# Layernorm, attention and ternary FFN on one core: head 1's keys and queries by seven block products, the second group's values in the lead-in

## The chip, the core and the metric

The kernel runs on 1 core of a Trainium2 chip. A core has TensorE (PE; its weight loads are listed as PEld), VectorE (DVE), ScalarE (ACT), GpSimd (POOL) and SyncE (SP, which here issues DMAs), an on-chip SBUF, and PSUM, where matmuls put their results. Each engine works through its own queue in order and waits on semaphores. The metric is device microseconds of one execution; before the change the median of 3 runs was 2255.35 us (2254.96 to 2256.19).

## What is computed

All in float32, with x of 2048 rows and 256 columns, 16 heads of 128, and a hidden FFN width of 704. The input x, of one batch, is normalized once; attention and FFN both read the normalized rows, and both are added to x.

```python
xn = _layernorm(x, axis=-1)
x = x + attn(xn, Wqkv, Wout) + ffn(xn, w1, w2, w3)

# attn
qkv = jnp.einsum('bsd,ed->bse', x, Wqkv).reshape(B, S, 3 * H, D)
q, k, v = qkv[:, :, :H], qkv[:, :, H:2 * H], qkv[:, :, 2 * H:]
logits = jnp.einsum('bqhd,bkhd->bhqk', q, k) * D ** (-0.5)
w = softmax(logits)
out = jnp.einsum('bhqk,bkhd->bqhd', w, v).reshape(B, S, H * D)
return jnp.einsum('bse,de->bsd', out, Wout)

# ffn: each weight matrix rounded to -1, 0, 1 times the rows
x1, x2 = _bitlinear(x, w1), _bitlinear(x, w2)
return _bitlinear(sigmoid(x1) * x2, w3)
```

## The kernel before

**Stages.** The front loads x and the first weights, normalizes x, and turns it into `xnT`, which has 128 of the 256 columns on the partitions twice (KC = 2), and all 2048 rows along it. In its gaps PE makes values of the first group of heads and queries of head 0. A group is G = 2 heads. Then the FFN runs over four chunks of 512 rows, with keys of head 0 between its first chunks. Then comes attention.

**Attention's loop.** A block is one head and 512 queries (NB = 4 blocks a head, 64 in all); a block has TB = 4 tiles of 128 queries. One turn of the loop at L733 makes the scores of tile v = u + 6 and the weighted sums of tile u, so that scores run LEAD = 6 tiles ahead. The turns with u < 0 (v = 0 to 5) are the lead-in: they have scores and no weighted sums, and other products fill PE instead, by the table `first` (L726). This text calls the turn that makes the scores of tile v "step v".

In a step, in this order: scores of tile v in two halves of 1024 keys (L602, two products each), a maximum of each half on DVE (L607) and the negated one of both (L612); `beside`, which may put a block product on PE and its read on DVE; the exponentials of both halves on ACT (L619); pieces of keys, queries or values; the first weighted sums (L660); a second block product; DVE's transposes of tile v - 2 (L650); the second product's read; the exchange of tile v by 16 DMAs of 64 KB (L634, ten on SP's queue, six on ACT's), which the transposes two steps later wait for; the remaining weighted sums. The order is written out by hand (`tc.manual_schedule`): each engine gets its instructions in the order of the program, and a DMA also waits for the DMA eight before it.

Score tiles have three buffers of two PSUM banks (`ps_s`). The other two banks are `ps_m` and `ps_av`, one buffer each. Pieces take their bank by `bank` (L87), in the lead-in and before by turns and later always `ps_m`, while block products always take `ps_m`:

```python
pool, tag = ((ps_m, "m"), (ps_av, "av"))[len(banks) % 2] if lead_in else (ps_m, "m")
banks.append(name)
```

**Pieces.** `k_piece` (L99) and `q_piece` (L111) make 128 x 512 of keys or queries by two products of 512 columns, which ACT copies out of PSUM (L109, L120). `v_piece` (L216) makes 256 rows of values for both heads of a group by four products of 256 columns, copied by ACT (L228). A float32 product is two instructions on PE. Head 0's keys and queries, and head 1's, are made by pieces: eight pieces of 512 columns a head. Head 1's fall into steps 1 to 4, 9 and 13.

**Seven block products.** For heads 2 to 15, keys and queries of two chunks of 512 rows are four outputs, each a sum of two products, eight in all; the kernel makes them by seven, from sums of weights (`weight_sums`, L133, POOL) and sums of x (`x_sums`, L143, POOL, once). `fast_product` (L151) puts one product into `ps_m`; `fast_read` (L168) adds it on DVE to one or two outputs (L185, L188, L192) and `fast_scaled` (L207) makes a scaled copy (L211). A pair of chunks is spread over four steps: (b, i) = (0,0), (0,1), (1,0) with two products each, (1,1) with one. Here b is the block in its pair and i the first or second tile of the block. A step with two has the first beside the scores and the second after some weighted sums. Values of groups 2 to 7 are made in a similar way (`fast_v_product`, L251).

**Around it.** `load_weights` (L72) starts a DMA of a group's weights. Each kind of weight has one buffer, so that a load waits until the last product that reads the old ones is done. Group 1's value weights are loaded in step 1 by SP, in its queue between the exchange of tile 0 with the FFN's last result (`yd`, L517) and the exchange of tile 1. Group 1's `wq` and `wk` are loaded by POOL in steps 12 and 14 (L81). `x_sums` are in step 1 and lie in a pool that takes the place of the FFN's.

Of the kernel before, what the change touches and what calls it, by code (L numbers as in the profile page):

```python
# [19 lines left out]
def layernorm_attention_bitffn_kernel(  # L20
# [78 lines left out]
    def k_piece(h: int, c: int):  # L99
        if c == 0:  # L100
            kTs[h] = kvpool.tile([P, S], F32, tag="kT", name=f"kT{h}")
        w = weights[h // G, "k"]
        pm = bank([P, QB], f"pk{h}_{c}")
        for d in range(KC):
            nc.tensor.matmul(  # L105
                pm, w[:, d, bass.ts(h % G, D)], xnT_k[:, d, c],
                start=(d == 0), stop=(d == KC - 1),
            )
        nc.scalar.copy(kTs[h][:, bass.ts(c, QB)], pm)  # L109
# [410 lines left out]
    with tc.manual_schedule():  # L520
        nc.gpsimd.memset(ones, 1.0)

        idle = ps_s.tile([P, 2, QB], F32, tag="s", name="idle")
        for i in range(20):
            nc.tensor.transpose(idle[:, i % 2, :P], ident, ident)
        with tc.tile_pool(name="fraw", bufs=1) as fraw:
            raw = loads(fraw)

            normalized(fraw, 0, 0, 2)
            turned(0, 0, 2)  # L530
            normalized(fraw, 0, 2, TB)
            v_piece(0, 0)
            turned(0, 2, TB)
            normalized(fraw, 1)
            q_piece(0, 0)
            v_piece(0, 1)
            turned(1, 0, 2)
            turned(1, 2, TB)
            normalized(fraw, 2)
            magnitude(fraw, 0, raw[0])  # L540
            v_piece(0, 2)
            q_piece(0, 1)
            magnitude_of_all(0)
            v_piece(0, 3)
            turned(2, 0, 2)
            turned(2, 2, TB)
            normalized(fraw, 3)
            quantize(fraw, 0, raw[0])
            magnitude(fraw, 1, raw[1])
            v_piece(0, 4)  # L550
            q_piece(0, 2)
            magnitude_of_all(1)
            turned(3)
            quantize(fraw, 1, raw[1])
            magnitude(fraw, 2, raw[2])
            v_piece(0, 5)
            v_piece(0, 6)
            q_piece(0, 3)
            magnitude_of_all(2)
            halved_x(0)  # L560
            quantize(fraw, len(raw) - 1, raw[-1])
        for c in range(2):
            k_piece(0, c)
        fp = front.enter_context(tc.tile_pool(name="ffn", bufs=2))
        chunks = [(c, f) for c in range(NB) for f in range(FC)]
        for i, (c, f) in enumerate(chunks):
            hidden(fp, c, f)
            if f == 2 and c + 1 < NB:
                halved_x(c + 1)
            if i < 2:  # L570
                k_piece(0, i + 2)
            else:
                summed(fp, *chunks[i - 2])
            if f == 3 and c:
                added(c - 1)

        warm = small.tile([P, 1], F32, tag="warm", name="warm", bufs=1)
        nc.scalar.activation(warm, ident[:, 0:1], AF.Exp)
# [139 lines left out]
    def put_away(n: int):  # L718
# [5 lines left out]
    GB = G * NB  # L724

    first = {  # L726
        1: [("v", 0, NV - 1), ("k", 1, 0)], 2: [("k", 1, 1), ("k", 1, 2)],
        3: [("k", 1, 3), ("q", 1, 0)], 4: [("q", 1, 1), ("v", 1, 0)], 5: [("v", 1, 1), ("v", 1, 2)],
    }
    made = {p for todo in first.values() for p in todo}  # L730
    moved = None
    with tc.manual_schedule():
        for u in range(-LEAD, (NBK - 1) * TB):  # L733
            n, t = divmod(u, TB)
            v = u + LEAD
            lead_in = u < 0
            more = v < NBK * TB
            h, b = blocks[v // TB] if more else (H, 0)


            seven = 2 <= h + 1 < H and v % TB < 2
            hi = h + 1, b, v % TB
            product, read, twice = fast_product, fast_read, (b % 2, v % TB) != (1, 1)

            if t == 0 and n >= GB and n // GB + 1 < H // G:
                seven = True
                hi = n // GB + 1, n % GB
                product, read, twice = fast_v_product, fast_v_read, n % NB != NB - 1


            moving = None
            if n >= GB and n // GB + 1 < H // G and n % NB > 1:
                moving = n // GB + 1, n % GB // NB, int(n % NB == 2)
            pms = []

            def beside():
                if v == 0:

                    for c, f in chunks[-2:]:
                        summed(fp, c, f)  # L760
                if seven:
                    pms.append(product(*hi, False))
                    read(*hi, False, pms[0])

            if more:
                scores(v, amid=(lambda: added(NB - 1)) if v == 1 else None, late=beside)

            if lead_in:
                for what, hg, i in first.get(v, ()):
                    {"q": q_piece, "k": k_piece, "v": v_piece}[what](hg, i)  # L770
                if v == 1:
                    front.close()
                    apool = ctx.enter_context(tc.tile_pool(name="apool", bufs=2))
                    load_weights(1, "v")
                    for c in range(0, NB, 2):
                        x_sums(c)
            elif t == 0:
                if n < GB and ("v", 1, n) not in made:
                    v_piece(1, n)
            elif t == 1:  # L780
                if n:
                    inverses(n - 1)
                    projected(n - 1, 0)
                if n % GB == GB - 1 and n // GB + 2 < H // G:
                    load_weights(n // GB + 2, "v")
            elif t == 2:
                if n and n % GB == 0:
                    load_weights(n // GB, "o", nc.gpsimd)
                if n % GB == GB - 1 and n // GB + 2 < H // G:
                    v_sums(n // GB + 2)  # L790
            if h == 0:
                if v % TB == 0 and ("k", 1, b) not in made:
                    k_piece(1, b)
                elif v % TB == 1 and ("q", 1, b) not in made:
                    q_piece(1, b)
            if b == NB - 1 and h + 2 < H:
                if h % G == 0 and v % TB in (0, 2):
                    load_weights(h // G + 1, "qk"[v % TB // 2], nc.gpsimd)
                if v % TB == 3:
                    weight_sums(h + 2)  # L800
            first_of_pair = product is fast_product and (b % 2, v % TB) == (0, 0)
            twice = seven and twice
            ahead = KQ // 2 if first_of_pair else KQ - 1
            if u >= 0:
                for k in range(t * KQ, t * KQ + ahead):
                    weighted(n, k)
            if twice:
                pms.append(product(*hi, True))
            if u == (NBK - 1) * TB - 1:
                inverses(NBK - 2)  # L810
                inverses(NBK - 1)
            if v > 1 and v - 2 < NBK * TB:
                transposed(v - 2)
            if twice:
                read(*hi, True, pms[1])
            if seven and first_of_pair:
                fast_scaled(h + 1, b)
            if more and t != TB - 1:
                exchanged(v)
            if u >= 0:  # L820
                for k in range(t * KQ + ahead, (t + 1) * KQ):
                    weighted(n, k)
            if more and t == TB - 1:
                exchanged(v)
            if u >= 0 and t == 1 and n:
                projected(n - 1, 1)
            if moving and t == 1:
                v_exchanged(*moving)
                moved = moving
            elif moved and t == 0:  # L830
                v_transposed(*moved)
                moved = None
            if t == 2 and n >= 0:
                if n:
                    put_away(n - 1)
                fetched(n)
                if n == NBK - 2:
                    fetched(NBK - 1)

        n = NBK - 1  # L840
        for k in range(NKT):
            weighted(n, k, 0)
            if k in (KQ - 1, 3 * KQ - 1):
                projected(n - 1, k // (2 * KQ), ps_s, "s")
        for k in range(NKT):
            weighted(n, k, 1)
            if k == KQ - 1:
                projected(n, 0, ps_m, "m")
        projected(n, 1, ps_s, "s")
# [38 lines left out]
```

## Time and profile before

| what | us |
|---|---|
| median of 3 runs (lowest, highest) | 2255.35 (2254.96, 2256.19) |
| the profiled execution, whole | 2257.09 |
| its span, from the first instruction to the last | 2255.3 |
| PE busy in the span | 2244.7 |
| DVE, ACT, POOL busy | 1681.3, 692.8, 317.8 |
| front and FFN, up to the first scores | 0 to 105.3 |
| lead-in, from the first scores to the first weighted sums | 105.3 to 152.1 |

The costliest groups of instructions; each row has the line, engine, operation, output and inputs, shapes and count, then busy us in all and mean ns of one, then idle us of the engine just before them and what ended it:

```profile
L619 ACT ACTIVATE p<-s,nm 128x1024 f32<-128x1024 f32 x512 | 566.0, 1110 | 1436.8 <-DMA part<-p 986.3
L607 DVE TENSOR_REDUCE mx<-s 128x1 f32<-128x1024 f32 x512 | 626.8, 1225 | 448.8 <-PE s L602 448.6
L660 PE MATMUL av<-pT,v 128*128 128x512 f32 (+1 forms) x2080 | 940.2, 586 | 0.7 <-DVE pT L650 0.7
L602 PE MATMUL s<-kT,qT 128*128 128x512 f32 x2048 | 921.9, 592 | 1.6 <-ACT p L619 1.5
L650 DVE STREAM_TRANSPOSE pT<-part 128x1024 f32<-128x1024 f32 x512 | 604.8, 1219 | 29.4 <-DMA part<-p 27.6
```

Matmuls overlap: the mean of 592 ns counts from the start of one to its own end, and the starts of two that follow each other are closer. In a timeline, a row gives start, us, engine, line, operation and count, and in brackets the idle time before it and what ended it. In a row of windows, each engine's busy us stands with its number of instructions; the granted TensorE clock (1.00 is full), the DMA engines' busy share and GB/s end the row.

### The profile page before, as it was taken

To read this page: it belongs to the slowest core of one execution; us is meant where nothing else is said; L and a number is where in the kernel's file an instruction comes from. 1 tells how busy PE (TensorE), PEld (TensorE's weight loads), DVE (VectorE), ACT (ScalarE), POOL (GpSimd) and SP (SyncE) were. 2 spreads that over 40 slices of the span, in tenths; PEclk is the share of its full clock that TensorE was granted. 3 is DMA by queue.
4 is the path that set the end of the run, shared out by engine and by line. 5 is a ranking of instruction groups with operands and counts; after the bars stand their busy time and mean duration, and the time that the engine had idled before them with its cause. 6 is when DMAs were issued, how large, how long until landed. Compare 5 with 4: busy or idle time off the path is not lost.

```text
span 2255.3 us, 24534 instructions
## 1 busy us (share of the span) xinstructions
PE 2244.7 (100%) x5754; PEld 1086.1 (48%) x5754; DVE 1681.3 (75%) x2205; ACT 692.8 (31%) x1203; POOL 317.8 (14%) x625
## 2 busy tenths in 40 slices
PE   9999999999999999999999999999999999999999
PEld 6744444444444444444444444444444444444445
DVE  6566777777777777777777777777777777777775
ACT  5533323223223223323323322322322322232331
POOL 0010000021030211203022120222103021120000
PEclk9999999999999999999999999999999999999999
DMA  2066665665665665666666665666666666666665
GB/s 95 28 164 160 171 162 147 175 176 151 166 182 152 180 174 149 177 173 167 160 175 157 176 181 147 166 179 173 168 159 174 166 174 164 157 176 173 168 170 155
DMA packets 237793, 364.73 MB, mean 162 GB/s; under 512 B 74576, under 2 KB 82192, under 8 KB 237648
## 3 DMA queue, kind: packets, MB, share of 16 engines
q1 hardware_dynamic: 131120, 178.36, 31.9%
q10 hardware_dynamic: 74704, 101.68, 17.8%
q0 software_dynamic: 31824, 83.13, 12.0%
q8 instruction: 45, 0.74, 0.1%
q14 instruction: 100, 0.82, 0.1%
HBM read 46.20 MB, written 35.65 MB: 36 GB/s over the span
## 4 chain that ended last, share of the span: by engine, by line
PE 94%; DMA 2%; SPq 1%; DVE 1%; ACT 1%; issue 0%; ACTq 0%; DVEq 0%
PE s L602 37%; PE av L660 37%; PE pw L165 7%; PE po L686 5%; PE pvw L263 3%; DMA part<-p 2%; PE ph L467 2%; PE pv L222 1%; PE pf L490 1%; SPq L634 1%; ACT p L619 0%; PE pq L115 0%; DVE pT L650 0%; PE pk L105 0%; ACTq L634 0%
## 5 line engine op out<-in xcount | busy, mean ns | idle before, releaser
L619 ACT ACTIVATE p<-s,nm 128x1024 f32<-128x1024 f32 x512 | 566.0, 1110 | 1436.8 <-DMA part<-p 986.3
L607 DVE TENSOR_REDUCE mx<-s 128x1 f32<-128x1024 f32 x512 | 626.8, 1225 | 448.8 <-PE s L602 448.6
L660 PE MATMUL av<-pT,v 128*128 128x512 f32 (+1 forms) x2080 | 940.2, 586 | 0.7 <-DVE pT L650 0.7
L602 PE MATMUL s<-kT,qT 128*128 128x512 f32 x2048 | 921.9, 592 | 1.6 <-ACT p L619 1.5
L650 DVE STREAM_TRANSPOSE pT<-part 128x1024 f32<-128x1024 f32 x512 | 604.8, 1219 | 29.4 <-DMA part<-p 27.6
L660 PEld LDWEIGHTS av<-pT,v 128*128 128x128 f32 x2080 | 395.1, 190 | 456.3 <-issue 449.9
L602 PEld LDWEIGHTS s<-kT,qT 128*128 128x128 f32 x2048 | 388.6, 190 | 464.8 <-issue 452.5
L287 POOL DMA_DIRECT2D xnT<-v x384 | 189.2, 501 | 346.5 <-DVE v L295 236.4
L721 POOL DMA_DIRECT2D yd<-ya x60 | 33.6, 560 | 735.3 <-DVE ya L693 734.0
L686 PE MATMUL po<-wo,oT 128*128 128x256 f32 x512 | 131.7, 380 | 0.6 <-DVE oT L669 0.5
L686 PEld LDWEIGHTS po<-wo,oT 128*128 128x128 f32 x512 | 97.0, 190 | 67.8 <-issue 58.4
L693 DVE SCALAR_TENSOR_TENSOR ya<-po,ri,ya 128x256 f32<-128x256 f32 x256 | 111.9, 479 | 18.0 <-issue 2.5
L619 ACT ACTIVATION_READ_ACCUMULATOR p<-s,nm 128x1 f32 x512 | 100.2, 196 | 0.0
L165 PE MATMUL pw<-t,ws 128*128 128x512 f32 x168 | 85.9, 593 | 0.0
L715 POOL DMA_DIRECT2D ya<-yd x64 | 34.3, 536 | 306.4 <-DMA yd<-ya 238.5
L188 DVE TENSOR_TENSOR kT<-pw,kT 128x512 f32<-128x512 f32 x112 | 74.7, 667 | 0.2 <-issue 0.2
L612 DVE TENSOR_REDUCE nm<-mx 128x1 f32<-128x2 f32 x256 | 39.7, 155 | 28.2 <-DVE mx L607 1.4
L185 DVE SCALAR_TENSOR_TENSOR qT<-pw,qT 128x512 f32<-128x512 f32 x84 | 57.4, 684 | 0.0
L165 PE MATMUL pw<-xnT,wk 128*128 128x512 f32 x112 | 57.2, 592 | 0.0
L280 DVE TENSOR_TENSOR v<-pvw,v 128x512 f32<-128x512 f32 x84 | 56.1, 680 | 0.0
L672 ACT COPY oT<-av 128x512 f32<-128x512 f32 x64 | 37.3, 583 | 59.2 <-PE av L660 53.6
L165 PEld LDWEIGHTS pw<-t,ws 128*128 128x128 f32 x168 | 31.6, 189 | 40.7 <-issue 33.7
(113 smaller groups left out, 784.8 us busy)
## 6 DMA issues: line engine op xcount, KB each, us to landing
part<-p SPq DMA_DIRECT2D x2560, 64.0 KB, 2.1
part<-p ACTq DMA_DIRECT2D x1536, 64.0 KB, 2.2
ya<-yd POOLq DMA_DIRECT2D x64, 512.0 KB, 4.2
yd<-ya POOLq DMA_DIRECT2D x60, 512.0 KB, 4.1
xnT<-v POOLq DMA_DIRECT2D x384, 32.0 KB, 2.6
wv<-in_wqkvT_dram SPq DMA_DIRECT2D x8, 256.0 KB, 3.6
yd<-y SPq DMA_DIRECT2D x4, 512.0 KB, 2.6
wq<-in_wqkvT_dram POOLq DMA_DIRECT2D x7, 256.0 KB, 3.7
```

The lines of the kernel that those rows point to most:

```text
L165: nc.tensor.matmul(pm, lhs, rhs, start=True, stop=True)
L185: nc.vector.scalar_tensor_tensor(q, pm, SCALE, base, ALU.mult, ALU.add)
L188: nc.vector.tensor_tensor(k, pk, base, ALU.add)
L263: nc.tensor.matmul(pm, lhs, rhs, start=True, stop=True)
L287: nc.gpsimd.dma_start(v_part[q // 2][bass.ts(j, 32), bass.ts(q % 2, S // 8)], v[bass.ts(q, 32), bass.ts(j, S // 8)],)
L602: nc.tensor.matmul(s[:, bass.ts(j, QB)], qTs[h, b][:, bass.ts(t, P)], kTs[h][:, i * HALF + j * QB : i * HALF + (j + 1) * QB], start=True, ...
L607: nc.vector.tensor_reduce(mx[:, i : i + 1], s, AX.X, ALU.max)
L619: nc.scalar.activation(p, s, AF.Exp, bias=nm, accum_out=sums[n][:, t, i : i + 1],)
L650: nc.vector.transpose(pTs[n][:, t, 2 * i : 2 * i + 2], part)
L660: nc.tensor.matmul(av, vs[h // G, k // (NKT // 2)][:, h % G, k % (NKT // 2), :], pTs[n][:, t0:t1].rearrange("p t g (k q) -> p (t g) k q", ...
L686: nc.tensor.matmul(pms[j], oTs[n, 2 * u + j], weights[h // G, "o"][:, h % G, :], start=True, stop=True,)
L693: nc.vector.scalar_tensor_tensor(y[:, t, :], pms[j], rinvs[n][:, t : t + 1], y[:, t, :], ALU.mult, ALU.add,)
```

## The change

Head 1's keys and queries are made by the seven block products too. In the lead-in, from step 3 on, a counter of its own spreads the first pair of chunks over steps 3 to 6; the second pair falls into steps 8, 9, 12 and 13 by the rule that the other heads have. All key and query pieces of head 1 go, and with them the lines that made them in the main loop. Of the values' pieces, the last of group 0 moves from step 1 into the front, and group 1's pieces 0 to 6 fill the lead-in (two each in steps 1 and 2, one each in steps 3, 4 and 5); before, 0 to 2 were in steps 4 and 5 and 3 to 7 in the main loop, where only the last, 7, is left. Group 1's value weights are loaded in the front, right after the moved piece, and the sums of head 1's weights are made on POOL after the FFN's instructions are recorded. A product's place in its pair is now told by `hi` instead of by b and v.

```diff
@@ -555,6 +555,8 @@
             magnitude(fraw, 2, raw[2])
             v_piece(0, 5)
             v_piece(0, 6)
+            v_piece(0, 7)
+            load_weights(1, "v")
             q_piece(0, 3)
             magnitude_of_all(2)
             halved_x(0)
@@ -573,6 +575,7 @@
                 summed(fp, *chunks[i - 2])
             if f == 3 and c:
                 added(c - 1)
+        weight_sums(1)
 
         warm = small.tile([P, 1], F32, tag="warm", name="warm", bufs=1)
         nc.scalar.activation(warm, ident[:, 0:1], AF.Exp)
@@ -724,8 +727,8 @@
     GB = G * NB
 
     first = {
-        1: [("v", 0, NV - 1), ("k", 1, 0)], 2: [("k", 1, 1), ("k", 1, 2)],
-        3: [("k", 1, 3), ("q", 1, 0)], 4: [("q", 1, 1), ("v", 1, 0)], 5: [("v", 1, 1), ("v", 1, 2)],
+        1: [("v", 1, 0), ("v", 1, 1)], 2: [("v", 1, 2), ("v", 1, 3)], 3: [("v", 1, 4)],
+        4: [("v", 1, 5)], 5: [("v", 1, 6)],
     }
     made = {p for todo in first.values() for p in todo}
     moved = None
@@ -738,9 +741,13 @@
             h, b = blocks[v // TB] if more else (H, 0)
 
 
-            seven = 2 <= h + 1 < H and v % TB < 2
+            seven = h + 1 < H and v % TB < 2
             hi = h + 1, b, v % TB
-            product, read, twice = fast_product, fast_read, (b % 2, v % TB) != (1, 1)
+            if v <= LEAD:
+
+                seven = v > 2
+                hi = 1, *divmod(v - 3, 2)
+            product, read, twice = fast_product, fast_read, hi[1] % 2 + hi[2] < 2
 
             if t == 0 and n >= GB and n // GB + 1 < H // G:
                 seven = True
@@ -767,11 +774,10 @@
 
             if lead_in:
                 for what, hg, i in first.get(v, ()):
-                    {"q": q_piece, "k": k_piece, "v": v_piece}[what](hg, i)
+                    v_piece(hg, i)
                 if v == 1:
                     front.close()
                     apool = ctx.enter_context(tc.tile_pool(name="apool", bufs=2))
-                    load_weights(1, "v")
                     for c in range(0, NB, 2):
                         x_sums(c)
             elif t == 0:
@@ -788,17 +794,12 @@
                     load_weights(n // GB, "o", nc.gpsimd)
                 if n % GB == GB - 1 and n // GB + 2 < H // G:
                     v_sums(n // GB + 2)
-            if h == 0:
-                if v % TB == 0 and ("k", 1, b) not in made:
-                    k_piece(1, b)
-                elif v % TB == 1 and ("q", 1, b) not in made:
-                    q_piece(1, b)
             if b == NB - 1 and h + 2 < H:
                 if h % G == 0 and v % TB in (0, 2):
                     load_weights(h // G + 1, "qk"[v % TB // 2], nc.gpsimd)
                 if v % TB == 3:
                     weight_sums(h + 2)
-            first_of_pair = product is fast_product and (b % 2, v % TB) == (0, 0)
+            first_of_pair = product is fast_product and hi[1] % 2 + hi[2] == 0
             twice = seven and twice
             ahead = KQ // 2 if first_of_pair else KQ - 1
             if u >= 0:
@@ -814,7 +815,7 @@
             if twice:
                 read(*hi, True, pms[1])
             if seven and first_of_pair:
-                fast_scaled(h + 1, b)
+                fast_scaled(*hi[:2])
             if more and t != TB - 1:
                 exchanged(v)
             if u >= 0:
```

`NV - 1` is 7; `TB` is 4; `LEAD` is 6. The functions called are unchanged.

## Prediction

> **What bounds the kernel now.** I read the page's busy shares first, then the windows of the lead-in, then the timeline of each engine there.
>
> ```profile
> PE 2244.7 (100%) x5754; PEld 1086.1 (48%) x5754; DVE 1681.3 (75%) x2205; ACT 692.8 (31%) x1203; POOL 317.8 (14%) x625
> ...
> 30.00:40.00 10.00, 10.00 (x36) 6.42 (x35) 7.22 (x12) 5.53 (x9) 0.00 (x0) 1.00 0.00 0
> ...
> 120.00:130.00 10.00, 9.46 (x22) 3.74 (x21) 6.20 (x6) 5.69 (x12) 5.05 (x5) 1.00 0.69 195
> 130.00:140.00 10.00, 10.00 (x27) 5.02 (x27) 6.35 (x7) 3.60 (x7) 5.54 (x5) 1.00 0.75 204
> 140.00:150.00 10.00, 8.95 (x31) 5.46 (x30) 7.23 (x7) 4.55 (x9) 0.00 (x0) 1.00 0.61 149
> ```
>
> PE is idle for only 10.6 us of the span. In the second kind of row (window, then busy us of PE, PEld, DVE, ACT and POOL) the front's 30 to 40 us is full and the lead-in lacks 0.54 and 1.05 us. So what counts is the work given to PE and what makes PE wait in the lead-in (105 to 149 us; steps are v of L735, from 0). PE's timeline of it:
>
> ```profile
> 122.57 3.60 PE L105 MATMUL pk<-xnT,wk 128*128 128x512 f32 x8
> 126.00 1.88 PE L602 MATMUL s<-kT,qT 128*128 128x512 f32 x4
> 128.32 1.98 PE L602 MATMUL s<-kT,qT 128*128 128x512 f32 x4 [0.44 <-ACT p L619]
> ...
> 143.39 1.98 PE L602 MATMUL s<-kT,qT 128*128 128x512 f32 x4 [1.05 <-ACT p L619]
> 145.21 3.62 PE L222 MATMUL pv<-wv,xnT 128*128 128x256 f32 x16
> 148.66 3.60 PE L602 MATMUL s<-kT,qT 128*128 128x512 f32 x8
> ```
>
> The scores of step 3 start at 126.00, those of step 6 at 148.66. One f32 product of 512 columns is two rows. The pace is 3.43 us per eight rows (the next start after 122.57), so 0.858 a product, 1.72 a piece, 3.43 the scores of a step. Between the two starts stand three scores and six pieces: 3 x 3.43 + 6 x 1.72 = 20.6 us of 22.66. **The old waits cost 2.05 us**, both for a score buffer that ACT's exponentials hold.
>
> **The change, part by part.**
>
> *Fewer products.* Head 1's keys and queries were 16 products, and become 14 (the built order has no key or query piece of head 1 left). 2 x 0.858 = **-1.72 us**, all on PE, which has no idle time where they are removed.
>
> *Moves that sum to nothing.* Values piece (0,7) goes into the front at 32.5 us, where PE is full: +1.72 there, -1.72 in step 1. Its ACT copy (0.585) finds ACT free 0.49 us before the next copy there, and both shift with PE. The remaining values pieces move from the main loop, full as well, to the lead-in.
>
> *The weights' load.* `wv` moves on SP's queue from 121.66 us, behind the last `yd`, to before the first `yd` (SP has nothing between 10.5 and 70.3). SP saves 0.50 us of issue. In step 1 ACT's last exchange issue waited until 126.41, and the exponentials of step 2 start at 127.06; the load landed at 125.95 between these transfers, against 124.38 for `yd` alone. I take 0.9 to 1.7 us earlier for the exponentials of steps 2 and 3. By that the first old wait goes. The second goes because PE will be later itself.
>
> *POOL.* Four weight sums (0.46 each) run early in an idle engine. The sums of x start when the last `yd` has landed (124.87) at 1.24 each; the two that step 3 needs are done by 127.4, seven us before their use. If they came seven later they would add to the waits below. `wq` of group 1 is released by step 9's product instead of the last query piece (205.80), `wk` by step 13's; their first use was at 227.96, ten us after they landed. The ten us cover it: nothing.
>
> *DVE.* A step has two maxima (1.225), one small maximum (0.15) and two transposes (2.37 together): 5.0 us of PE's 6.86. Step 3 adds 0.68, 0.67 and 0.43, steps 4 and 5 up to 2.0. It fits in the sum; the order is what costs.
>
> *The new waits.* A product goes to the single bank of `ps_m`. In the built order step 3 is: scores, first product (bank m), values piece 4 (bank m), second product (bank m). Step 5 is the same with piece 6. Step 4's piece takes the other bank. So in steps 3 and 5 the piece waits for DVE's read, and the second product for ACT's copy of the piece, which stands behind that step's exponentials. The main loop shows how long the read takes after the scores:
>
> ```profile
> 227.96 1.02 PE L165 MATMUL pw<-xnT,wk 128*128 128x512 f32 x2
> 228.82 1.88 PE L660 MATMUL av<-pT,v 128*128 128x512 f32 x4
> ...
> 228.16 1.22 DVE L607 TENSOR_REDUCE mx<-s 128x1 f32<-128x1024 f32 x1 [0.49 <-PE s L602]
> 229.50 0.15 DVE L612 TENSOR_REDUCE nm<-mx 128x1 f32<-128x2 f32 x1
> 229.57 0.68 DVE L192 COPY kT<-pw 128x512 f32<-128x512 f32 x1
> ```
>
> The scores end at 227.96, the bank is read by 230.25: 2.3 us later. There four rows of `av` fill the time; in the lead-in nothing does.
>
> Step 3, from E, the end of its scores (126.00 + 3.43 = 129.43): bank free at E + 2.37, piece until E + 4.1. ACT: exponentials at 133.56 in the old run, less 0.9 to 1.7, take 2.2, then the copy 0.59: second product at E + 5.2 to E + 6.0. Without waits it is E + 0.86 + 1.72 = E + 2.58. Lost: **2.6 to 3.4**. Step 5 reads twice (0.68 + 0.67): bank free at E + 3.05, piece until E + 4.8, copy after 0.2 + 0.6: E + 5.6. Lost: **3.0**; here PE is so late that ACT is ready. Each of four restarts costs 0.1 more (1.98 for a row that otherwise takes 1.88): 0.4. Step 4: its second product waits for a read at E + 2.4 and comes at E + 2.6: nothing. Step 6's product stands behind 3.4 us of scores: nothing.
>
> Bounds: ACT quite free in step 3 gives E + 4.9, lost 2.35; ACT not earlier at all gives E + 7.0, lost 4.4. Sum: -1.72 - 2.05 + 2.6..3.4 + 3.0 + 0.4 = 2.2 to 3.0, with the bounds 2.0 to 4.1. I take **+2.8 us**, near the side where only `wv`'s 0.9 is saved.
>
> *The clock.* Idle stretches this dense were seen once, in the front:
>
> ```profile
> 5.30:8.70 3.40, 1.93 (x11) 1.00 1.01 321
> 8.70:12.10 3.40, 3.40 (x11) 0.51 1.06 389
> ```
>
> PE was busy for 57% of one stretch of 3.4 us, no gap over 0.80, and ran at half the granted clock (the column after PE's busy time) in the next. The lead-in's worst stretch now, 141.9 to 145.3, has 1.05 idle (69% busy) and kept 1.00. The new waits leave some 55% in step 3 (idle 1.5 and 1.9 around a piece of 1.72) and 40 to 50% in step 5 (2.2 and 0.85). A stretch of 3.4 at half clock loses up to 1.7; I take 1.4, as waits fall into it. Bounds: none, and two, 3.4.
>
> [...]
>
> **Cases.** The profiled execution took 2257.09 with a span of 2255.3, the median is 2255.35; differences of the span are put on the median. A difference of 0.2% is 4.5 us.
>
> *Forecast, 0.45: the bank waits and one or two half-clock stretches.* One gives 2259.6, two 2261.0; I name **2260.0**. Its own range is 2258.8 to 2262.9 (+4.1 + 3.4).
>
> *Waits alone, 0.35.* The clock holds: 2258.2 (2257.3 to 2259.5). For it: threshold unknown between 57 and 69%, and the front's rows were short transposes.
>
> *Not slower, 0.12.* The exchange paces the lead-in: exponentials start at 119.49 in step 1 and 155.14 in step 6, 7.13 a step against PE's 6.86, so PE's waits might only use slack behind it, and the load taken off SP pays them. Then only the two products count: 2255.35 - 1.72 = 2253.6. It decides if the new waits stay within the old 2.05; against it stands 2.3 us of DVE per read, whose order no exchange changes.
>
> *DVE feeds back, 0.08.* The second read stands behind transposes that wait for the exchange (DVE waited 2.17 at 140.87). If the exchange of step 2 lands after 142, the wait delays the next maxima, exponentials and exchange, in steps 4, 5 and 6: 3 x 2.17 = 6.5 more, 2264.7 and up. Against: by then PE is four us later than the exchange.
>
> The range 2253.5 to 2262.5 leaves out half of the third case, the last and the top of the first: about 0.17. Slower by over 0.2% (above 2259.9): two stretches 0.20, a third of the single ones and some of the second case 0.14, the last 0.08: 0.42. Faster by over 0.2% needs 4.5 and the whole gain without any new wait is 3.8: 0.03, for what I haven't seen. Within: 0.55.
>
> **What would show it.** PE idle of 1.4 or more before `pv` L222 twice between 128 and 153 us, released by DVE; before `pw` L165 twice, released by ACT's `v` copy; none before `s`. The scores of step 6 some 4.5 to 8 us later than 148.66 after the front's 1.72 is taken off. A granted clock below 1.00 around 135 or 152. Head 1's products at steps 8 to 13 without PE idle. It is wrong if the copy of values piece 4 or 6 comes before the exponentials, if PE loses under 2 us there, or if the main loop shows new idle time.

## The result and the profile after

| kernel | executions | median us (lowest to highest) | ratio to before, 95% interval |
|---|---|---|---|
| before | 22 | 2254.93 (2253.08 to 2256.61) | |
| changed | 22 | 2257.87 (2255.67 to 2261.77) | 1.0014 [1.0008, 1.002] |

The change costs 2.9 us, 0.13%. That is under the 0.2% that was set as the bound, but the interval lies wholly above 1. The forecast was 2260.0, the range 2253.5 to 2262.5.

The page of the changed kernel: first PE's busy us and instructions, then two groups.

```profile
PE 2241.4 (99%) x5750; PEld 1084.9 (48%) x5750; DVE 1692.4 (75%) x2223; ACT 689.0 (31%) x1195; POOL 319.8 (14%) x629
...
L663 PE MATMUL av<-pT,v 128*128 128x512 f32 (+1 forms) x2080 | 940.7, 586 | 1.1 <-DVE pT L653 1.1
L605 PE MATMUL s<-kT,qT 128*128 128x512 f32 x2048 | 920.9, 592 | 0.0
```

PE has four rows fewer, the two products that were saved. Before the scores (L605 now) nothing is waited for any more; they had 1.6 us. PE's idle time is nevertheless 13.2 us of the span of 2254.6, where it was 10.6 of 2255.3. These two spans can't be set against each other directly: the profiled execution of before ran a stretch of its front at half clock (0.51 from 8.70 to 12.10, the rows in the prediction), the one of after did not (1.00 up to 2253.49); its whole time, 2256.51, is one of the lower ones of its 22.

The timeline of PE in the lead-in of the changed kernel, from the scores of step 3 to those of step 6:

```profile
125.76 3.60 PE L605 MATMUL s<-kT,qT 128*128 128x512 f32 x8
129.19 1.02 PE L165 MATMUL pw<-xnT,wk 128*128 128x512 f32 x2
131.46 1.99 PE L222 MATMUL pv<-wv,xnT 128*128 128x256 f32 x8 [1.25 <-DVE kT L192]
134.22 1.10 PE L165 MATMUL pw<-t,ws 128*128 128x512 f32 x2 [0.76 <-POOL t L148]
135.15 3.60 PE L605 MATMUL s<-kT,qT 128*128 128x512 f32 x8
...
142.03 3.60 PE L605 MATMUL s<-kT,qT 128*128 128x512 f32 x8
145.46 1.02 PE L165 MATMUL pw<-t,ws 128*128 128x512 f32 x2
148.40 1.99 PE L222 MATMUL pv<-wv,xnT 128*128 128x256 f32 x8 [1.92 <-DVE kT L188]
151.07 1.13 PE L165 MATMUL pw<-xnT,ws 128*128 128x512 f32 x2 [0.68 <-ACT v L228]
152.03 3.60 PE L605 MATMUL s<-kT,qT 128*128 128x512 f32 x8
```

Two waits in step 3, two in step 5, none in step 4. From 125.76 to 152.03 are 26.27 us with the same 20.6 us of work as before: 5.67 lost instead of 2.05. The list of PE's waits from 20 to 2240 us (total, times, longest) has nothing else beyond 0.3 us in the front:

```profile
PE pv L222 <- DVE kT L188: 1.9, 1, 1.9
PE pv L222 <- DVE kT L192: 1.2, 1, 1.2
PE pw L165 <- POOL t L148: 0.8, 1, 0.8
PE pw L165 <- ACT v L228: 0.7, 1, 0.7
```

What stands behind the second waits is seen on ACT, whose copy of the piece (L228) comes after the two exponentials (L622) of the step:

```profile
131.34 1.11 ACT L622 ACTIVATE p<-s,nm 128x1024 f32<-128x1024 f32 x1 [3.25 <-DMA part<-p]
...
132.45 1.11 ACT L622 ACTIVATE p<-s,nm 128x1024 f32<-128x1024 f32 x1
...
133.54 0.58 ACT L228 COPY v<-pv 128x512 f32<-128x512 f32 x1
...
150.43 0.59 ACT L228 COPY v<-pv 128x512 f32<-128x512 f32 x1 [0.90 <-PE pv L222]
```

In step 3 the piece ends at 133.45, the copy at 134.12, and the second product starts 0.10 later; in step 5 the copy ends at 151.02 and the product starts at 151.07. The copies start 0.09 and 0.04 after their pieces end, so the exponentials hold them up by next to nothing in this execution; what is lost is the chain of DVE's read, the piece and its copy. The first waits end with DVE's reads, the second of step 5's two being the later:

```profile
130.73 0.68 DVE L192 COPY kT<-pw 128x512 f32<-128x512 f32 x1
...
147.07 0.68 DVE L185 SCALAR_TENSOR_TENSOR qT<-pw,qT 128x512 f32<-128x512 f32 x1
147.66 0.68 DVE L188 TENSOR_TENSOR kT<-pw,kT 128x512 f32<-128x512 f32 x1
```

**The sum.** 3.6 us more lost in the lead-in, less 1.72 for two products, is 1.9. The 22 executions, sorted by their mean granted clock, show the rest:

| mean granted clock | executions | median us |
|---|---|---|
| 1.000 | 9 | 2256.89 |
| 0.999 | 6 | 2258.02 |
| 0.998 | 7 | 2260.11 |

At full clock the changed kernel is 2256.89 - 2254.93 = 1.96 slower, near the 1.9 of the trace. The two agree better than the data allow: 2254.93 is the median over all clocks, the nine executions spread over 1.9 us, and with both kernels at 1.000 on one chip the difference is 2257.28 - 2255.54 = 1.74. PE's time for the same work in the main loop, from the scores of step 6 to the last sums ahead of its wait near the end, also differs between executions: 2086.50 us here (152.03 to 2238.53), 2087.21 in e1's second run below (147.74 to 2234.95). The other 1.0 of the median goes with the clock, which is under 1.000 in 13 of 22 executions. Of 33 executions of the kernel before, on one chip, 28 have 1.000, five 0.999 and none 0.998.

### The profile page after: what moved, and what is told of

Read it like the earlier page. It is cut to its first block, busy times and chain, and to the rows that moved or that the text cites. A ratio compares the mean times of both kernels' runs of the same rounds, so it can differ in the third digit from the quotient of the medians.

```text
span 2254.6 us, 24539 instructions
## 1 busy us (share of the span) xinstructions
PE 2241.4 (99%) x5750; PEld 1084.9 (48%) x5750; DVE 1692.4 (75%) x2223; ACT 689.0 (31%) x1195; POOL 319.8 (14%) x629
## 4 chain that ended last, share of the span: by engine, by line
PE 97%; DMA 1%; DVE 1%; SPq 0%; ACT 0%; issue 0%; ACTq 0%; DVEq 0%
PE s L605 38%; PE av L663 38%; PE pw L165 8%; PE po L689 5%; PE pvw L263 3%; PE ph L467 2%; PE pv L222 1%; DMA part<-p 1%; PE pf L490 1%; SPq L637 0%; PE pq L115 0%; PE pk L105 0%; ACT p L622 0%; DVE pT L653 0%; DVE mx L610 0%
## 5 line engine op out<-in xcount | busy, mean ns | idle before, releaser
L622 ACT ACTIVATE p<-s,nm 128x1024 f32<-128x1024 f32 x512 | 566.0, 1110 | 1436.8 <-DMA part<-p 949.1
L605 PE MATMUL s<-kT,qT 128*128 128x512 f32 x2048 | 920.9, 592 | 0.0
L605 PEld LDWEIGHTS s<-kT,qT 128*128 128x128 f32 x2048 | 389.0, 190 | 462.0 <-issue 454.8
L622 ACT ACTIVATION_READ_ACCUMULATOR p<-s,nm 128x1 f32 x512 | 100.2, 196 | 0.0
L165 PE MATMUL pw<-t,ws 128*128 128x512 f32 x180 | 92.0, 592 | 0.8 <-POOL t L148 0.8
L188 DVE TENSOR_TENSOR kT<-pw,kT 128x512 f32<-128x512 f32 x120 | 80.1, 667 | 3.5 <-PE pw L165 3.3
```

The source lines that it names most:

```text
L165: nc.tensor.matmul(pm, lhs, rhs, start=True, stop=True)
L188: nc.vector.tensor_tensor(k, pk, base, ALU.add)
L605: nc.tensor.matmul(s[:, bass.ts(j, QB)], qTs[h, b][:, bass.ts(t, P)], kTs[h][:, i * HALF + j * QB : i * HALF + (j + 1) * QB], start=True, ...
L622: nc.scalar.activation(p, s, AF.Exp, bias=nm, accum_out=sums[n][:, t, i : i + 1],)
```

## The experiments

All were compared with the kernel before on the same chip. The first four, on one chip, had its median at 2255.61, the other four, on another, at 2255.06.

| run | what is different | median us (lowest to highest) | ratio to before, 95% interval |
|---|---|---|---|
| c0_after | the changed kernel again | 2258.16 (2256.54 to 2260.1) | 1.0012 [1.0003, 1.0021] |
| e1_other_bank | pieces never in the products' bank | 2252.9 (2251.59 to 2254.56) | 0.9987 [0.9978, 0.9996] |
| e2_same_bank | pieces always in it | 2260.58 (2259.09 to 2262.78) | 1.0022 [1.0013, 1.0031] |
| e3_kept_busy | waits filled with transposes | 2256.47 (2255.54 to 2258.62) | 1.0003 [0.9994, 1.0012] |
| e4_load_alone | kernel before, early load alone | 2254.81 (2253.87 to 2257.36) | 1.0 [0.9991, 1.0009] |
| e5_later_sums | half of POOL's sums later | 2258.48 (2255.86 to 2262.14) | 1.0014 [1.0005, 1.0023] |
| e1b_other_bank | e1 again, on the other chip | 2252.49 (2251.76 to 2254.08) | 0.9989 [0.998, 0.9998] |
| e6_front_warm | e1 with a busier PE in the front | 2252.68 (2251.73 to 2253.99) | 0.9989 [0.998, 0.9997] |

**The changed kernel again**, without an edit, as what the next three are set against.

> The changed kernel itself, beside the others on one chip. Theory (the bank waits cost some 5 us of PE in steps 3 and 5, and in part of the executions a half-clock stretch comes on top): the median is near 2257.9, and executions with a mean clock of 0.998 lie 2 to 4 us over those with 1.000. Rival (the executions differ by the exchange, not by the clock): the times spread without regard to the clock.

It came to 2258.16; six of 11 executions had clock 1.000 (median 2257.28), three 0.999, and two 0.998, which lie 2.8 over the six, as the theory has it.

**Pieces in the other bank.** From step 3 to the end of the lead-in every piece takes `ps_av`, which the weighted sums don't need yet.

```diff
+        if forced:
+            pool, tag = forced[0]
...
+                if v == 3:
+                    forced.append((ps_av, "av"))
```

> From step 3 on, the values pieces of the lead-in take the other bank. Theory: the four idle times of PE (1.25, 0.76, 1.92, 0.68) and their restarts go, all but some 0.5 where a read of two outputs ends after the piece, and perhaps 0.3 for a score buffer; 4 to 4.5 us less than the changed kernel, 2253.4 (2252.5 to 2254.2), below the kernel before, and no execution with a clock of 0.998. Rival (the exchange paces the lead-in): PE waits for the exponentials instead, and the time stays within 1 us of the changed kernel's.

It came to 2252.9, 5.26 under the control, where 4 to 4.5 were expected. Among executions at 1.000 the difference is 4.40 (2252.88 and 2257.28); the rest goes with the clock, and no execution had 0.998. PE's timeline of this kernel in steps 3 and 5 (its line numbers are two higher):

```profile
130.78 1.02 PE L167 MATMUL pw<-xnT,wk 128*128 128x512 f32 x2
131.64 1.89 PE L224 MATMUL pv<-wv,xnT 128*128 128x256 f32 x8
133.36 1.02 PE L167 MATMUL pw<-t,ws 128*128 128x512 f32 x2
134.22 3.60 PE L607 MATMUL s<-kT,qT 128*128 128x512 f32 x8
...
147.52 1.13 PE L167 MATMUL pw<-xnT,ws 128*128 128x512 f32 x2 [0.19 <-DVE kT L190]
```

Product, piece, product and scores follow each other without a gap; only step 5's second product waits, 0.19. So the waits belong to the one bank, and it isn't the exchange that paces the lead-in: with the waits gone PE simply goes faster. There is not much room behind it, though: in the profile of this kernel's second run (e1b) the scores of step 5 wait 0.71 for exponentials. POOL in this kernel:

```profile
134.06 1.27 POOL L150 TENSOR_TENSOR t<-xnT,t 128x512 f32<-128x512 f32 x1
```

It is the last of the sums, and ends at 135.33, two us after the product at 133.36 has started. That product reads the second of the eight sums, which ends at 127.86 here and at 125.90 in the changed kernel. In the changed kernel the profile names POOL (L148) for the 0.76 before the same product, but it is ACT's copy that was late.

**Pieces in the same bank.** The same edit with `ps_m`, so that step 4 shares the bank too.

```diff
-                    forced.append((ps_av, "av"))
+                    forced.append((ps_m, "m"))
```

> From step 3 on, all values pieces of the lead-in take the products' bank, piece 5 in step 4 too. Theory: step 4 gets the waits that steps 3 and 5 have, 1.25 before the piece and some 0.7 before the second product, with restarts 2.2 us more than the changed kernel: 2260.1 (2259.3 to 2261.5). Rival (exchange): at most 0.5 more.

It came to 2260.58, 2.4 over the control. PE's timeline in steps 4 and 5:

```profile
141.03 1.99 PE L224 MATMUL pv<-wv,xnT 128*128 128x256 f32 x8 [1.32 <-DVE qT L187]
143.79 1.10 PE L167 MATMUL pw<-t,wq 128*128 128x512 f32 x2 [0.77 <-ACT v L230]
...
151.09 3.19 PE L224 MATMUL pv<-wv,xnT 128*128 128x256 f32 x8 [1.92 <-DVE kT L190]
154.96 2.08 PE L167 MATMUL pw<-xnT,ws 128*128 128x512 f32 x2 [0.68 <-ACT v L230]
156.83 4.46 PE L607 MATMUL s<-kT,qT 128*128 128x512 f32 x8
```

Step 4 now has the same pair of waits (1.32 and 0.77). The piece of step 5 takes 3.19 us where it took 1.99 in the changed kernel, the second product 2.08 for 1.13: the clock. The windows of PE in the same execution (window, length, busy us, granted clock, DMA share, GB/s):

```profile
144.90:148.30 3.40, 3.40 (x9) 1.00 0.80 190
148.30:151.70 3.40, 1.48 (x6) 1.00 0.28 66
151.70:158.50 6.80, 6.12 (x11) 0.50 0.52 123
```

After a window with 1.48 us of work (44%), whose longest gap was the 1.92 us wait, the clock is 0.50 for 6.8 us. In the clock records of the kernel before the stretches are 3.413 and 3.413 us in the front and then 2242.556, which is 657 times 3.4133; the changed kernel's is 2245.970, 658 times; the 6.8 here are two. So the windows of each trace are laid in steps of 3.413 us from its changes of the clock. The changed kernel has the same wait in step 5, of the same 1.92, and kept its clock:

```profile
147.48:150.90 3.42, 1.99 (x8) 1.00 0.42 100
150.90:154.31 3.41, 3.24 (x8) 1.00 0.78 185
```

Its wait began at 146.48, a microsecond before the window, so 1.99 us of work (58%) fell into it. Had the window begun with the wait, it would have held 3.41 - 1.92 = 1.49, as in this run. Where the windows lie differs from one profile to the next. The control and e5 (below) have the wait of 1.92 too, and there as well a border between two windows cuts it; in each, this is the emptier of the two windows:

```profile
146.84:150.25 3.41, 1.80 (x8) 1.00 0.65 154
...
144.90:148.31 3.41, 1.79 (x5) 1.00 0.62 153
```

With 53% (the control) and 52% (e5) busy both kept their clock in the next window too. So of four profiles with this wait, the one whose window takes in the whole of it lost the clock. That this is what sorts the 22 executions fits with these four, but was not shown by itself.

**Waits filled.** PE transposes a constant into the other bank while it waits, in steps 3 and 5; the results are not read.

```diff
+    def keep(m: int):
+        it = ps_av.tile([P, QB], F32, tag="av", name=f"keep{v}_{m}")
+        for i in range(m):
+            nc.tensor.transpose(it[:, bass.ts(i % 4, P)], ident, ident)
...
+                if v in (3, 5):
+                    keep(13 if v == 3 else 19)
...
+                if v in (3, 5):
+                    keep(7)
```

> PE does transposes of the identity into the free bank while it waits in steps 3 and 5 (13 and 7, then 19 and 7); nobody reads them. Theory (half-clock stretches after the waits): the waits stay, the stretches go, so no execution is over 2258.5 or shows a clock under 0.999, and the median falls by about 1 us to 2256.9. Rival (the clock has no part in the lead-in): median 2257.9 and the spread up to 2261 stay.

It came to 2256.47, 1.69 under the control, where about 1.0 was expected; the two intervals overlap. One execution, at 2258.62, lay just outside what was expected of all. None had 0.998, and four had 0.999. The profiled one is of these four, and its half clock lies in the front, not in the lead-in:

```profile
4.60:8.02 3.42, 1.81 (x12) 1.00 0.98 323
8.02:11.43 3.41, 3.41 (x9) 0.50 1.07 385
```

The profile of the kernel before, at 0.999 as well, also has its half clock in the front, 0.50 from 8.74 to 12.15; in that of e1, at 0.999 too, no product of the lead-in is slowed from step 3 on (1.02 to 1.13 us for its two rows, where e2's has 2.08). So a 0.999 can be the front's, which the kernel before has too, and it is 0.998 that goes with the waits of the lead-in: 16 of 54 executions of the kernels with these waits (changed, control, e2, e5) have 0.998 or less, and none of the 121 others whose clock is on record. PE's timeline of step 5 and of the last weighted sums:

```profile
147.13 1.02 PE L165 MATMUL pw<-t,ws 128*128 128x512 f32 x2
147.99 2.24 PE L737 MATMUL keep<-ident 128*128 128x128 f32 x19
150.06 1.99 PE L222 MATMUL pv<-wv,xnT 128*128 128x256 f32 x8
...
2240.44 4.02 PE L663 MATMUL av<-pT,v 128*128 128x256 f32 x16
```

Step 5's piece starts 2.93 us after its first product, against 2.94 in the changed kernel: the wait is as long, but PE is busy in it. The executions at 1.000 are 1.33 under those of the control all the same (2255.95 and 2257.28). A part lies at the end of the kernel, where the sums of the last row run through, while the changed kernel had a gap of 1.1:

```profile
2241.51 1.99 PE L663 MATMUL av<-pT,v 128*128 128x256 f32 x8 [1.09 <-DVE pT L653]
```

That wait is 0.7 in the kernel before, 1.5 in e1 and 1.7 in its second run; what sets it stays open. Since 1.33 of the 1.69 us remain at equal clock, only about 0.4 can be put to the clock. That the 0.998 executions go when the waits are filled is shown; the 1.0 expected of the median is not.

**The early load alone.** The kernel before, with values piece (0,7) and the load of `wv` in the front.

```diff
             v_piece(0, 6)
+            v_piece(0, 7)
+            load_weights(1, "v")
...
-        1: [("v", 0, NV - 1), ("k", 1, 0)], 2: [("k", 1, 1), ("k", 1, 2)],
+        1: [("k", 1, 0)], 2: [("k", 1, 1), ("k", 1, 2)],
...
-                    load_weights(1, "v")
```

> The kernel before with one part of the change alone: values piece (0,7) in the front and group 1's value weights loaded right behind it; head 1 still by pieces. Theory: the exponentials of step 2 start some 2 us earlier after the start of their scores' stage, but PE now reaches step 3 with 1.72 us less work behind it, so that one wait for a score buffer (1 to 1.5, in step 5) stays; 0.3 to 1.0 less than the kernel before, not measurably more. Rival (the load among the exchange is the cause of both old waits): both go, 2.0 less than the kernel before.

It came to 2254.81, 0.25 under the kernel before and inside the uncertainty. The first old wait is gone from its trace; the second is left, 1.00 instead of 1.05:

```profile
124.03 3.60 PE L604 MATMUL s<-kT,qT 128*128 128x512 f32 x8
...
140.65 1.98 PE L604 MATMUL s<-kT,qT 128*128 128x512 f32 x4 [1.00 <-ACT p L621]
...
2216.51 1.98 PE L604 MATMUL s<-kT,qT 128*128 128x512 f32 x4 [0.96 <-ACT p L621]
```

The last row is a wait near the end of the kernel that the kernel before doesn't have (e6, below, has one of 1.43 at 2214.75); it takes back what the first one gave. So the early load, together with the moved piece, releases the first old wait alone; the second is gone in the changed kernel, where PE is late itself, as predicted.

**Half of POOL's sums later.** This was to tell whether POOL had released the 0.76.

```diff
-                    for c in range(0, NB, 2):
-                        x_sums(c)
+                    x_sums(0)
+                if v == 5:
+                    x_sums(2)
```

> The changed kernel with the sums of x for the second pair of chunks made in step 5 instead of step 1, so that POOL is done with the first pair's by 128.5. Theory (the second product of step 3 waits for ACT's copy out of its bank): the 0.7 to 0.8 us before it stay, the time is the changed kernel's, 2257.9 (2257.2 to 2258.6). Rival (it waits for POOL, as the profile names it): that wait goes, 0.9 less, 2257.0.

It came to 2258.48, but the edit did not do what it was meant to: POOL has nothing else in its queue there, and worked through the sums at the same time as before, until 133.9. The wait stayed, on PE:

```profile
134.43 1.10 PE L165 MATMUL pw<-t,ws 128*128 128x512 f32 x2 [1.30 <-POOL t L148]
```

and ACT's copy ended 0.10 ahead of it:

```profile
133.75 0.58 ACT L228 COPY v<-pv 128x512 f32<-128x512 f32 x1
```

The wait is longer than the 0.76 because the copy started 0.63 after its piece had ended (133.12), directly behind the exponentials. On POOL's part this run separates nothing by itself; e1's POOL row does.

**The better version again, and with a busier front.** The second adds six transposes ahead of each of two places in the front, so that PE's first stretches are not half empty.

```diff
+            for i in range(6):
+                nc.tensor.transpose(idle[:, i % 2, :P], ident, ident)
             turned(0, 0, 2)
             normalized(fraw, 0, 2, TB)
+            for i in range(6):
+                nc.tensor.transpose(idle[:, i % 2, :P], ident, ident)
             v_piece(0, 0)
```

> The kernel with the pieces in the other bank once more, as a control on this chip: 2252.9, 2.7 less than the kernel before (0.9978 to 0.9996 of it).

> The same, and PE does six transposes of the identity in each of two gaps of the front (before the first real transposes and before the first values piece). Theory (a stretch with 57% of PE's time busy ahead of the next one costs the clock there too): the half clock behind the front's gaps goes in most executions, 0.5 to 1.0 less on the median than the control. Rival (the front is paced by DVE and ACT there): no difference over 0.3.

They came to 2252.49 and 2252.68: no gain, where 0.5 to 1.0 was expected. All 11 executions of e6 had 1.000, but so had ten of e1b's 11. The front's half-clock stretch, which the profile of before happened to catch, is too rare to be worth anything in the median. The version with the pieces in the other bank beats the kernel before twice, by 2.6 to 2.7 us, 0.11 to 0.13%, and the changed one by more.

## Why the prediction was right, and where it was off

**Two products fewer, -1.72: right.** PE has four rows fewer, and the lead-in's 3.6 less this term gives 1.9, beside 1.96 and, on one chip, 1.74 measured at full clock.

**The old waits, -2.05: right.** No score waits in the lead-in. The load from SP's queue was to bring the exponentials 0.9 to 1.7 us forward; those of step 2 start at 124.83 instead of 127.06, 2.2 earlier, though their scores start at the same time (118.88 and 118.77).

**The new bank waits: the mechanism right, step 3 a little too dear.** Predicted were four waits, of these places and releasers, and none in step 4. Step 3's second product was to come 5.2 to 6.0 us after the end of the scores; it came at 134.22 - 129.19 = 5.03, a loss of 2.45 instead of 2.6 to 3.4, because ACT was earlier still. Step 5's came at 5.61, predicted 5.6, a loss of 3.03. Of the 5.67 lost that leaves 0.19 for the restarts, predicted 0.4. By themselves the terms gave +2.8 us; 1.96 was measured, just under the bound of 2.0. (The upper bound, 4.1, adds up to 4.0.) Two of the signs named beforehand were missed by this: the first wait was 1.25 instead of 1.4 or more, and the scores of step 6 came 3.6 later after those of step 3, not 4.5 to 8. That the shared bank is the cause is shown from both sides: without it -5.3, with one sharing step more +2.4.

**The clock: the step that failed.** One row of the front, 57% busy and then half clock, was taken as the rule for the median: +1.4 for one stretch or +2.8 for two, on top of the +2.8 of the waits. In the profiled execution both windows with the waits were 58% busy and kept 1.00, and the control's, 53% busy, kept it too; a threshold of the busy share between 57 and 69% is not shown. What was forecast for the kernel is true of a share of its executions: seven of 22 have 0.998 and lie 3.2 over those at 1.000. In e2's trace that is two windows, both behind step 5; step 3's waits kept 1.00 in all four profiles that have them unfilled. The six at 0.999, 1.1 over, can in part be the front's. The forecast of 2260.0 is the median of the seven (2260.11). That of the whole, 2257.87, is below that case's own range, from 2258.8, and near the 2258.2 of the waits alone, but by luck: the waits gave 1.96 instead of 2.8, and the clock, which that case leaves out, the other 1.0. The whole range is 9 us wide and holds the time of the kernel before as well, so that the time lies inside it says little for the forecast case.

**The rivals.** That the exchange paces the lead-in fell with e1, 5.3 us faster with the same exchange; the 0.71 in its second run is what is left of it. That DVE's second read delays the following steps didn't come: after 152 us PE has no wait until the last twenty us. The covers costed at nothing (POOL's sums, the loads of `wq` and `wk`, step 4's second product, steps 8 to 13) held: none appears in the list of waits.

## What to carry to other kernels

Before a filler is put beside a product, look at which bank each will take: two that shared a bank here made PE wait 1.25 and 1.92 us for DVE's read of the first, and 0.76 and 0.68 for ACT's copy, and a reader also stood behind what its own engine had to do first (in e5 ACT's copy started 0.63 after its piece had ended, directly behind the exponentials); the choice of the bank was worth 5.3 us, 4.4 of it at equal clock, more than the 1.72 of the products that the change saved. Where a saving is small, price the waits of its new order from the readers' queues, step by step; that sum was good to 1 us. The clock loss expected from one row of one profile was here true of a share of the executions (0.998 in seven of 22), not a term of the sum, and is best read from the granted clocks of many.

## What the hardware showed unexpectedly

The granted clock halved after windows of about 3.4 us that were only partly empty: 44% busy in e2 and 57% in the front of the kernel before, with no gap over 1.92 and 0.80 us. The busy share that the profile counts doesn't sort the cases: after 53% (the front of e3) the clock halved as well (0.50), after 53% (the control), 52% (e5) and twice 58% (the changed kernel), all in the lead-in, it stayed at 1.00. What else counts is open. In the clock records of the kernel before and of the changed one the stretches were 3.413, 3.413, 2242.556 and 2245.970 us long, 1, 1, 657 and 658 times 3.4133. The clock stayed at half for one such window in the fronts (3.41 us in the kernel before and in e3) and for two in e2 (6.8 us; PE was busy for 2.73 us of the first). The same 1.92 us wait cost the clock in one profile and not in three others, and the executions of the changed kernel spread over 6.1 us, those of the kernel before over 3.5.

For one wait of the changed kernel the profile named a releaser that had been done for 0.82 us: POOL, whose last sum (L148) ended at 133.40, for a product that started at 134.22, 0.10 after ACT's copy had ended (134.12).
